# A second one-hot product for the virtual tiles of a graph network, and a shorter gather list

## The chip, the cores and the metric

The kernel runs on one NeuronCore of a Trainium2 chip. The metric is the device time of one execution in microseconds (us). TensorE is called PE here, VectorE DVE, ScalarE ACT, GpSimd POOL and SyncE SP, as in the profile.

## What is computed

Three GraphSAGE layers with maximum aggregation run on 6250 nodes and 200000 edges; the edges are sorted by destination, and low destination numbers have many edges. Cut to what matters:

```
def _sage_conv(x, src, dst, Wl, bl, Wr):
    agg = jax.ops.segment_max(x[src], dst, num_segments=x.shape[0])
    agg = jnp.where(jnp.isfinite(agg), agg, 0.0)
    return agg @ Wl + bl + x @ Wr

h = jnp.maximum(_layernorm(x, axis=-1), 0.0)
h = leaky_relu(_sage_conv(h, ...))   # 128 -> 256
h = leaky_relu(_sage_conv(h, ...))   # 256 -> 256
h = leaky_relu(_sage_conv(h, ...))   # 256 -> 128
return x + h
```

For every node, each layer needs the maximum over the feature rows of its sources.

## The kernel before

**Tiles and pairs.** Nodes are cut into 50 tiles of 127. As sources, two neighbouring tiles make a pair, so there are 25 pairs (`NG`). As destinations, tiles become units of 128 columns in four groups (`GROUPS`, L93): group 0 has 24 narrow units, group 1 has 8 virtual units, group 2 has 19 wide units, group 3 has 4 narrow units. The virtual units stand for the first three tiles, whose nodes have so many edges that each node is cut into rows of up to 64 edges (`CUT`); 8 units hold these rows, and after group 1 the class `Joined` takes the maximum over the rows of one node.

**Two ways to fetch a source row.** The first way is a product: for a pair and a unit, a matrix with a single one per column picks one row of the pair, and PE multiplies the pair's features with it, in two parts (`i`) for exactness. A narrow unit takes one edge per pair in this way: the two tiles of the pair (`s`) are two halves of one sum, and DVE takes one maximum of the result into the accumulator (`maxima`, L929). A wide or virtual unit takes one edge per tile: the two halves are separate results, with a maximum each. ACT builds the one-hot matrices from the index bytes with two instructions each (`one_hot`, L897: Square at L902, Relu at L904), for up to 1024 columns at a time (`HOT`). The second way is a list: the edges left over go to one of four lists (`CAPS`, one per group), sorted so that the deepest rows come first. Each entry is a gather, an indirect DMA that POOL issues for 128 rows (`Listed.gather`, L961, the DMA at L970, followed by a short memset at L974 that paces the queue). DVE takes the maxima of the gathered rows (L985, L990), in blocks of eight gathers in layer 0 and of four in layers 1 and 2.

**Order.** The program is one list of steps written out by hand (`steps`, L1110). For each layer and group the 25 pairs are gone through, and within a pair the chunks of the group: 1024 columns per step in layer 0, where a row is 128 features wide, and 512 columns per step in layers 1 and 2, where it is 256. This gives 75, 25, 75 and 25 steps for the four groups in layer 0, and 150, 50, 125 and 25 in layers 1 and 2. A full step has 8 matmuls of 512 columns (L921). Each step's work goes out in one fixed order on each engine: the products of half 0, then what an agenda has for this step (maxima of gathers, the stages of finished nodes, new gathers), then half 1 and the maximum.

**The agenda.** Everything that is not a product is planned on step numbers. The gathers of lists 0 to 2 are spread evenly from the layer's start to six or eight steps before the end of group 2; in layers 1 and 2 a wide or virtual step counts 1.25 and a narrow one 1.0 (`WIDER`). List 3 goes with group 3. The nodes of a group are finished while the next group runs: for each tile its gathered maximum is fetched (L1014), transposed, merged with the accumulator, and multiplied with the weights (`Node`, L997). For the 24 tiles of group 0 one node begins per step in layer 0, and one per two steps in layers 1 and 2, so they fill the steps of group 1. The eight virtual units and their three tiles follow in the first steps of group 2.

**Building the lists.** The edge rows are read and masked; `flag_rows` (L500) marks which edges the products do not take, `pick_rows` (L531) takes them out eight at a time, `rank_rows` (L549) orders the rows by how many are left, `send_row` scatters them. `expand` (L697) finds, for five pairs at a time, the edge a product takes, and `lookups` (L717) turns that into the index bytes (`idx`). For lists 1 to 3 this is done as chores on the agenda during the first 82 steps of layer 0; those of list 1 lie in the first 40.

If a list or a window should turn out too small for the input, counters (`over`) send the program to a slow general path at its end (L1376).

The stages named in the prediction were found by counting the matmuls of L921 in the order of time: 600, 200, 500 and 100 for the four groups of layer 0, and 1200, 400, 1000 and 200 in layers 1 and 2. They are exact to a few us.

Of the kernel before, what the change touches and what calls it, by code (L numbers as in the profile page):

```python
# [35 lines left out]
I32 = mybir.dt.int32  # L36
# [6 lines left out]
P = 128  # L43
# [6 lines left out]
CUT = 64  # L50
# [10 lines left out]
DEEP = (24, 40, 48, 24)  # L61
# [7 lines left out]
def kernel(ctx: ExitStack, tc: tile.TileContext, x, src, dst,  # L69
# [28 lines left out]
    )  # L98
    PLACE, HEAD = {}, []
# [42 lines left out]
    IW = [(len(units) + sum(w == "w" for w, _ in units)) * P for units in GROUPS]  # L142
# [226 lines left out]
    rows_w = edge.tile([P, NW + NV, 2 * CUT], I16, name="rows_w")  # L369
    pos_i = edge.tile([P, NV], I32, name="pos_i")  # L370
# [90 lines left out]
    def rows_of(us):  # L461
        w, i = us[0]
        assert [u for u in us] == [(w, i + j) for j in range(len(us))]
        return (rows_n if w == "n" else rows_w)[:, i : i + len(us), :]
# [35 lines left out]
    def flag_rows(us, S):  # L500
# [23 lines left out]
        one_less = slice(0, J - 1)  # L524
        nc.vector.tensor_scalar(f[:, :, one_less], b[:, :, one_less], 0.0, float(LEAF), op0=OP.not_equal, op1=OP.mult)
# [191 lines left out]
    def lookups(us, least, s, pool, tags=("v", "v8")):  # L717

        n = len(us)
        wide = us[0][0] == "w"  # L720
        v = pool.tile([P, n, NG], BF16, tag=tags[0], name="v", bufs=1 + (tags[0] == "v"))
        nc.vector.scalar_tensor_tensor(v, least, float(P if wide else 2 * P), least, op0=OP.is_lt, op1=OP.mult)
        if s:
            nc.vector.tensor_scalar(v, v, float(P), None, op0=OP.add)
        v8 = pool.tile([NG, n * P], U8, tag=tags[1], name="v8", bufs=1 + (tags[0] == "v"))
        i = 0
        while i < n:
            k = next(k for k, units in enumerate(GROUPS) if us[i] in units)
            m = 1
            while i + m < n and m < 8 and us[i + m] in GROUPS[k]:  # L730
                m += 1
            p = psum.tile([NG, 8, P], BF16, tag=next(turns), name="lk_p")
            for c in range(m):
                nc.tensor.transpose(p[:, c, :], v[:, i + c, :], ident_b)
            part = v8[:, i * P : (i + m) * P]
            nc.scalar.copy(part.rearrange("g (c k) -> g c k", k=P), p[:, :m, :])
            at = GROUPS[k].index(us[i]) + (len(GROUPS[k]) if s else 0)
            nc.sync.dma_start(idx[k][:, at * P : (at + m) * P], part)
            stored[k] += m * P
            i += m  # L740
# [114 lines left out]
    def chunks(layer, k):  # L855

        n = 8 if widths[layer] == P else 4
        units = GROUPS[k]
        for w in "wn":
            us = [i for i, u in enumerate(units) if u[0] == w]  # L860
            for i0 in range(0, len(us), n):
                part = us[i0 : i0 + n]
                yield (HEAD[k] + part[0]) * P, len(part) * P, part[0], units[part[0]][1] if w == "w" else None
# [23 lines left out]
    def parts_of(k):  # L887

        units = GROUPS[k]
        for w in "wn":  # L890
            us = [i for i, u in enumerate(units) if u[0] == w]
            for i0 in range(0, len(us), HOT // P):
                yield us[i0], len(us[i0 : i0 + HOT // P]) * P, len(units) if w == "w" else 0
# [3 lines left out]
    def one_hot(layer, k, g, c, w, odd, s):  # L897

        t, of = idx_q[layer, k, g]
        at = of + (c + (odd if s else 0)) * P  # L900
# [28 lines left out]
    def maxima(step, s, p, acc):  # L929
        layer, k, g, (_, w, c, odd_u) = step  # L930
# [4 lines left out]
        if g == NG - 1 and (odd_u is None or s == 0):  # L935
# [218 lines left out]
    def late_lookups(us, s):  # L1154
        got = {}
        for g0 in range(0, NG, BATCH):
            def part(g0=g0):
                if g0 == 0:
                    got[0] = made.tile([P, len(us), NG], I16, tag="least", name="least", bufs=2)
                expand(us, CUT if us[0][0] == "w" else CB, g0, s, got[0], S_acc)  # L1160
# [5 lines left out]
    late_lookups(LISTS[1], 1)  # L1166
    n_soon = len(chores)
# [481 lines left out]
```

## Time and profile before

| what | value |
|---|---|
| time, median of 3 runs | 3579.78 us (3576.79 to 3585.17) |
| the profiled execution's own time | 3583.85 us |
| its span, first to last instruction | 3582.1 us |
| mean granted PE clock | 0.86 of full |
| gathers of the lists (L970) | 1815, that is 605 per layer |
| one-hot matrices (L904) | 1200 |
| matmuls with one-hot matrices (L921) | 7000 |
| maxima of products (L938 and L936) | 1350 |
| moved by DMA | 579.84 MB |

Times in the profile are of one execution. A row of a group gives the line of the kernel, the engine, the operation, the tiles written and read, how often it ran, its busy time and the mean of one, and then how long its engine was idle just before such instructions, and what ended that. A row of the stage table gives a stretch of the span from its start, its length, the busy time of each engine with the number of its instructions, the granted PE clock, the share of the DMA engines' time and the rate in GB/s.

### The profile page before, as it was taken

The numbers are of one execution on the slowest core, as the hardware profiler recorded it, in microseconds if no ns is written. First come the engines' busy times: TensorE is split into PE (matmuls) and PEld (weight loads), VectorE is DVE, ScalarE is ACT, GpSimd is POOL, SyncE is SP. The second block draws the span as 40 slices with busy tenths as digits, with TensorE's granted clock in tenths as the row PEclk, the third lists the DMA queues.
The fourth block names the chain that finished last, engine by engine and source line by source line (L and its number), as shares of the span: only waits on it lengthen the run. The fifth ranks groups of instructions, "written<-read, shape, count | busy, mean of one in ns | idle before, by whom it ended". The sixth has DMA issues, their size and how long they took to land.

```text
span 3582.1 us, 37453 instructions
## 1 busy us (share of the span) xinstructions
PE 2378.9 (66%) x8912; PEld 1680.0 (47%) x8912; DVE 2594.4 (72%) x4077; ACT 2460.1 (69%) x3433; POOL 2837.5 (79%) x4030
## 2 busy tenths in 40 slices
PE   1025632557567567888778687769888777677767
PEld 1013421334334335666555455547666555455545
DVE  6557899987556535666667899955666678799964
ACT  5108952769779758998655587757998856477754
POOL 5578894888888873888876788883888888878884
PEclk9986865769767779999889899989999989899989
DMA  9114320338644366555577665578555567565566
GB/s 288 43 20 111 100 76 14 93 98 265 155 129 125 109 188 184 157 171 159 183 227 233 174 186 175 167 212 281 163 162 165 157 212 239 159 168 171 172 188 195
DMA packets 295272, 579.84 MB, mean 162 GB/s; under 512 B 58529, under 2 KB 155669, under 8 KB 294403
## 3 DMA queue, kind: packets, MB, share of 16 engines
q1 hardware_dynamic: 203331, 347.72, 29.7%
q0 software_dynamic: 91648, 229.44, 24.6%
q8 instruction: 75, 1.23, 0.1%
q14 instruction: 154, 1.26, 0.1%
q10 hardware_dynamic: 64, 0.20, 0.0%
HBM read 486.57 MB, written 90.55 MB: 161 GB/s over the span
## 4 chain that ended last, share of the span: by engine, by line
POOL 27%; DVE 22%; PE 14%; issue 14%; ACT 10%; DMA 10%; another core or an unknown queue 1%; SPq 1%; POOLq 0%; DVEq 0%; ACTq 0%
POOL g L970 18%; DVE acc L938 8%; PE pg L921 8%; POOL pace_t L974 7%; ACT sq L902 6%; DMA g<-table,let 5%; ACT hot L904 3%; PE z_p L1043 2%; DVE g L985 2%; DVE g L990 1%; PE z_p L1045 1%; DVE acc L541 1%; DVE acc L539 1%; DMA agg<-best,end_i 1%
## 5 line engine op out<-in xcount | busy, mean ns | idle before, releaser
L921 PE MATMUL pg<-hot,pair_sb 128*128 128x512 f32 x7000 | 2045.9, 440 | 540.3 <-DVE acc L938 243.4
L970 POOL DMA_INDIRECT g<-table,let x1815 | 1830.8, 1009 | 451.0 <-issue 285.2
L921 PEld LDWEIGHTS pg<-hot,pair_sb 128*128 128x128 f32 x7000 | 1397.5, 212 | 1050.5 <-ACT hot L904 293.7
L938 DVE TENSOR_TENSOR acc<-acc,pg 128x1024 f32<-128x1024 f32 (+3 forms) x1314 | 1488.5, 1161 | 309.0 <-PE pg L921 205.9
L904 ACT ACTIVATE hot<-sq 128x1024 fp32r<-128x1024 bf16 (+2 forms) x1200 | 1126.5, 939 | 367.8 <-PE pg L921 298.4
L902 ACT ACTIVATE sq<-idx_sb,near 128x1024 bf16<-128x1024 uint8 (+2 forms) x1200 | 1218.7, 1016 | 15.5 <-POOL pace_t L974 15.5
L974 POOL MEMSET pace_t<- 128x300 bf16 x1815 | 664.0, 366 | 0.9
L985 DVE TENSOR_TENSOR g<-g 128x1024 f32<-128x1024 f32 (+4 forms) x277 | 290.6, 1049 | 209.9 <-DMA g<-table,let 192.8
L1047 ACT COPY s<-z_p 127x256 f32<-127x256 f32 (+1 forms) x150 | 49.9, 333 | 368.4 <-PE z_p L1045 230.6
L990 DVE TENSOR_TENSOR g<-g 128x256 f32<-128x256 f32 (+3 forms) x355 | 175.7, 495 | 83.1 <-DMA g<-table,let 55.9
L1014 POOL DMA_INDIRECT agg<-best,end_i x141 | 140.5, 997 | 95.2 <-PE aT_p L1030 35.5
L959 ACT ACTIVATE let<-ell 128x4 int32<-128x4 int16 (+3 forms) x516 | 92.8, 189 | 86.9 <-DMA ell<-picks 86.9
L1030 PE MATMUL aT_p<-ident,agg 128*128 128x128 f32 x250 | 57.7, 297 | 141.4 <-DMA agg<-best,end_i 112.2
L1043 PE MATMUL z_p<-wr,hT_in 128*128 128x256 f32 (+1 forms) x500 | 148.6, 418 | 4.6 <-DMA hT_in<-across 4.5
L1036 DVE TENSOR_TENSOR mz<-acc,aT_p 128x256 f32<-128x256 f32 (+1 forms) x141 | 52.4, 371 | 131.3 <-PE aT_p L1030 89.3
L1045 PE MATMUL z_p<-wl,mz 128*128 128x256 f32 (+1 forms) x500 | 121.1, 359 | 8.0 <-DVE mz L1036 3.6
L1030 PEld LDWEIGHTS aT_p<-ident,agg 128*128 128x128 f32 x250 | 34.3, 148 | 170.2 <-DMA agg<-best,end_i 114.6
L605 POOL DMA_INDIRECT picks<-picked,to_i x55 | 59.3, 1078 | 64.7 <-DVE rank_h L581 48.1
L1043 PEld LDWEIGHTS z_p<-wr,hT_in 128*128 128x128 f32 x500 | 86.9, 217 | 34.2 <-issue 12.7
L1045 PEld LDWEIGHTS z_p<-wl,mz 128*128 128x128 f32 x500 | 92.3, 210 | 20.9 <-DVE mz L1036 4.4
L830 PE MATMUL hT_p<-ident,h 128*128 128x128 f32 x200 | 44.9, 309 | 82.8 <-DVE mz L1036 44.3
L348 POOL DMA_INDIRECT win_d<-in_dst_dram,win_i x50 | 52.3, 1046 | 44.0 <-ACT junk_w L353 14.7
(259 smaller groups left out, 1133.5 us busy)
## 6 DMA issues: line engine op xcount, KB each, us to landing
pair_sb<-pair SPq DMA_DIRECT2D x200, 512.0 KB
idx_sb<-idx SPq DMA_DIRECT2D x75, 608.0 KB
g<-table,let POOLq DMA_INDIRECT x1815
idx_sb<-idx SPq DMA_DIRECT2D x75, 384.0 KB
pair_sb<-pair SPq DMA_DIRECT2D x100, 256.0 KB
pair<-pr SPq DMA_DIRECT2D x100, 256.0 KB
idx_sb<-idx SPq DMA_DIRECT2D x75, 256.0 KB
best<-g SPq DMA_DIRECT2D x110, 128.0 KB
```

The lines of the kernel that those rows point to most:

```text
L902: nc.scalar.activation(sq[:, :w], t[:, at : at + w], AF.Square, bias=near[:, s : s + 1], scale=1.0)
L904: nc.scalar.activation(hot[:, :w], sq[:, :w], AF.Relu, bias=1.0, scale=-1.0)
L921: nc.tensor.matmul(to, pr[:, s, i, kk * P : (kk + 1) * P], hot[:, o : o + bw], start=((alone or s == 0) and i == 0), stop=((alone or s == ...
L938: nc.vector.tensor_max(to, to, of)
L959: nc.scalar.activation(let[:, :n], ell[self.k][:, q, j : j + n], AF.Identity, scale=1.0)
L970: nc.gpsimd.indirect_dma_start(out=self.tiles[q, b][:, i, :], out_offset=None, in_=tables[self.layer], in_offset=bass.IndirectOffsetOnAxis ...
L974: nc.gpsimd.memset(pace_t, 0.0)
L985: nc.vector.tensor_max(base[:, : i + 1, :], base[:, : i + 1, :], g[:, : i + 1, :])
L990: nc.vector.tensor_max(base[:, :h, :], base[:, :h, :], base[:, w - h : w, :])
L1014: nc.gpsimd.indirect_dma_start(out=self.agg[:, : self.F], out_offset=None, in_=of, in_offset=bass.IndirectOffsetOnAxis(ap=at, axis=0),)
L1043: nc.tensor.matmul(z_p, self.hT[:, i, :], wr[layer][:, i, :], start=False, stop=False)
L1045: nc.tensor.matmul(z_p, self.m[:, i, :], wl[layer][:, i, :], start=False, stop=(i == K - 1))
```

## The change

The eight virtual units get a second kind of product. `flag_rows` looks, among the edges that the first product leaves over, for one per pair; these go to new rows (`rows_x`) and are masked out of the list. New units `("x", v)` are appended to group 1 for the steps and for the index bytes (`PLANES`), while the lists and accumulators stay with `GROUPS`. An x unit is treated as a narrow one: the two halves are one sum, with one maximum, into the accumulator columns of virtual unit v. The list of group 1 has caps of 22, 15, 14, 12, 11, 9, 2 and 1, together 86, in place of 37, 30, 29, 27, 26, 23, 8 and 1, together 181; its depth falls from 40 to 24, so `pick_rows` runs three rounds per unit there and not five. One more set of `expand` and `lookups` is added to the chores, behind those of list 1.

```
-    (37, 30, 29, 27, 26, 23, 8, 1),
+    (22, 15, 14, 12, 11, 9, 2, 1),
...
-DEEP = (24, 40, 48, 24)
+DEEP = (24, 24, 48, 24)
...
+    EXTRA = [("x", v) for v in range(NV)]
+    PLANES = [units + (EXTRA if k == 1 else []) for k, units in enumerate(GROUPS)]
...
-    IW = [(len(units) + sum(w == "w" for w, _ in units)) * P for units in GROUPS]
+    IW = [(len(units) + sum(w == "w" for w, _ in units)) * P for units in PLANES]
...
+        if wide and us[0][1] >= NW:
+            c, seen = S(1, I32, n, J), S(2, I32, n, J)
+            nc.vector.memset(b[:, :, J - 1 :], 0)
+            nc.vector.tensor_copy(c, b)
+            repeated(seen, c, J)
+            nc.vector.tensor_tensor(b, b, c, op=OP.bitwise_xor)
+            x = rows_of([("x", i - NW) for _, i in us])
+            nc.vector.tensor_scalar(f, b, 0.0, float(PAST), op0=OP.is_equal, op1=OP.mult)
+            nc.vector.tensor_tensor(x, f, r[:, :, :J], op=OP.max)
+            nc.vector.tensor_scalar(f, b, 0.0, float(PAST), op0=OP.not_equal, op1=OP.mult)
+            nc.vector.tensor_tensor(r[:, :, :J], f, r[:, :, :J], op=OP.max)
+            b = c
...
     def chunks(layer, k):
...
-        units = GROUPS[k]
-        for w in "wn":
+        units = PLANES[k]
+        for w in "wnx":
...
-                yield (HEAD[k] + part[0]) * P, len(part) * P, part[0], units[part[0]][1] if w == "w" else None
+                yield part[0] - (NV if w == "x" else 0), len(part) * P, part[0], units[part[0]][1] if w == "w" else None
...
     def maxima(step, s, p, acc):
-        layer, k, g, (_, w, c, odd_u) = step
+        layer, k, g, (c, w, _, odd_u) = step
...
-        if g == NG - 1 and (odd_u is None or s == 0):
+        if g == NG - 1 and c == step[3][2] and (odd_u is None or s == 0):
...
     late_lookups(LISTS[1], 1)
+    late_lookups(EXTRA, 0)
     n_soon = len(chores)
```

The remaining edits carry the new units through `lookups`, `parts_of` and `one_hot`, so that the x columns lie behind the 16 of the virtual units in the index bytes. Group 1 then has 50 steps in layer 0 in place of 25, and 100 in place of 50 in layers 1 and 2; per layer 95 gathers go.

More of the change, by code (lines that the diff above doesn't have):

```diff
@@ L369 @@
     rows_w = edge.tile([P, NW + NV, 2 * CUT], I16, name="rows_w")
+    rows_x = edge.tile([P, NV, CUT], I16, name="rows_x")
     pos_i = edge.tile([P, NV], I32, name="pos_i")
@@ L463, in rows_of @@
         assert [u for u in us] == [(w, i + j) for j in range(len(us))]
-        return (rows_n if w == "n" else rows_w)[:, i : i + len(us), :]
+        return {"n": rows_n, "w": rows_w, "x": rows_x}[w][:, i : i + len(us), :]
     def count_of(us):
@@ L727, in lookups @@
         while i < n:
-            k = next(k for k, units in enumerate(GROUPS) if us[i] in units)
+            k = next(k for k, units in enumerate(PLANES) if us[i] in units)
             m = 1
-            while i + m < n and m < 8 and us[i + m] in GROUPS[k]:
+            while i + m < n and m < 8 and us[i + m] in PLANES[k]:
                 m += 1
@@ L736, in lookups @@
             nc.scalar.copy(part.rearrange("g (c k) -> g c k", k=P), p[:, :m, :])
-            at = GROUPS[k].index(us[i]) + (len(GROUPS[k]) if s else 0)
+            at = NV + PLANES[k].index(us[i]) if us[i] in EXTRA else GROUPS[k].index(us[i]) + (len(GROUPS[k]) if s else 0)
             nc.sync.dma_start(idx[k][:, at * P : (at + m) * P], part)
@@ L887, in parts_of @@
     def parts_of(k):
-        units = GROUPS[k]
-        for w in "wn":
+        units = PLANES[k]
+        for w in "wnx":
             us = [i for i, u in enumerate(units) if u[0] == w]
             for i0 in range(0, len(us), HOT // P):
-                yield us[i0], len(us[i0 : i0 + HOT // P]) * P, len(units) if w == "w" else 0
+                yield us[i0], len(us[i0 : i0 + HOT // P]) * P, len(GROUPS[k]) if w == "w" else 0
     hots, live, done_with = {}, [0], [0, 0]
@@ L899, in one_hot @@
         t, of = idx_q[layer, k, g]
-        at = of + (c + (odd if s else 0)) * P
+        at = of + (c + (odd if s else 0) + (NV if PLANES[k][c] in EXTRA else 0)) * P
         sq = work.tile([P, HOT], BF16, tag="sq", name="sq", bufs=2)
@@ L1159, in part @@
                     got[0] = made.tile([P, len(us), NG], I16, tag="least", name="least", bufs=2)
-                expand(us, CUT if us[0][0] == "w" else CB, g0, s, got[0], S_acc)
+                expand(us, CB if us[0][0] == "n" else CUT, g0, s, got[0], S_acc)
             chores.append((.7 * len(us), part))
```

## The prediction

> **What bounds the kernel now.** I read the page first, then the stage table, then the waits and the order of instructions inside stages.
>
> ```profile
> PE 2378.9 (66%) x8912; PEld 1680.0 (47%) x8912; DVE 2594.4 (72%) x4077; ACT 2460.1 (69%) x3433; POOL 2837.5 (79%) x4030
> ...
> POOL 27%; DVE 22%; PE 14%; issue 14%; ACT 10%; DMA 10%; another core or an unknown queue 1%; SPq 1%; POOLq 0%; DVEq 0%; ACTq 0%
> ```
>
> POOL is the busiest engine and has the largest share of the chain that ended last, but four engines lie between 66% and 79%, so the average decides nothing. The stage table does (columns: stretch, length, then PE, PEld, DVE, ACT, POOL busy, clock, DMA share, GB/s). The rows are, in this order, groups 0, 1 and 2 of layer 0, of layer 1 and of layer 2.
>
> ```profile
> 287.00:743.00 456.00, 224.88 (x653) 141.61 (x654) 404.51 (x1023) 323.69 (x373) 362.50 (x531) 0.71 0.27 75
> 743.00:898.00 155.00, 102.36 (x378) 65.97 (x379) 120.22 (x254) 125.53 (x181) 128.44 (x179) 0.83 0.68 201
> 898.00:1236.00 338.00, 206.01 (x570) 132.54 (x569) 192.29 (x251) 280.87 (x402) 297.03 (x435) 0.72 0.45 128
> 1350.00:1728.00 378.00, 311.37 (x1236) 239.83 (x1236) 241.58 (x263) 339.70 (x408) 295.39 (x431) 0.92 0.55 163
> 1728.00:1958.00 230.00, 177.06 (x675) 126.72 (x673) 162.03 (x190) 123.02 (x183) 173.78 (x243) 0.86 0.72 220
> 1958.00:2344.00 386.00, 294.13 (x1102) 202.38 (x1102) 358.40 (x361) 277.47 (x398) 328.86 (x476) 0.93 0.60 178
> 2465.00:2837.00 372.00, 318.90 (x1295) 247.19 (x1294) 242.17 (x258) 336.36 (x407) 288.53 (x422) 0.95 0.56 168
> 2837.00:3034.00 197.00, 142.00 (x644) 103.25 (x643) 160.61 (x193) 114.58 (x150) 172.35 (x236) 0.92 0.69 221
> 3034.00:3429.00 395.00, 297.00 (x1094) 203.62 (x1094) 357.94 (x360) 272.75 (x385) 341.08 (x488) 0.90 0.57 167
> ```
>
> Group 0 of layer 0 is DVE's (405 of 456 us, the chores). Group 0 of layers 1 and 2 has ACT first (340 of 378) with POOL behind it. Group 2 has DVE at 93% and 91% in layers 1 and 2. POOL's true load is higher than its busy time, since every gather has an idle gap of issue before it:
>
> ```profile
> 1647.28 0.95 POOL L970 DMA_INDIRECT g<-table,let  x1 [0.16 <-issue]
> ...
> 1648.76 0.95 POOL L970 DMA_INDIRECT g<-table,let  x1 [0.17 <-issue]
> ```
>
> One gather to the next is 1.48 us. Two stretches of group 0 in layer 1 show what that does: the early part with all engines, then both parts with the one-hots of L904 alone, then the waits from 1540 to 1728.
>
> ```profile
> 1400.00:1500.00 100.00, 89.14 (x357) 68.95 (x356) 69.94 (x67) 98.53 (x113) 87.55 (x130) 0.95 0.55 158
> ```
>
> ```profile
> 1400.00:1500.00 100.00, 48.93 (x47) 0.95 0.55 158
> 1540.00:1720.00 180.00, 78.45 (x74) 0.94 0.54 159
> ```
>
> ```profile
> DVE g L985 <- DMA g<-table,let: 41.8, 16, 5.4
> PE pg L921 <- DVE acc L938: 28.4, 14, 3.6
> ...
> POOL g L970 <- issue: 18.3, 107, 0.9
> ```
>
> Early, ACT is busy 98.5 of 100 us and makes 47 one-hots, 2.13 us each, one per step: that is ACT's own pace. Later a step takes 180/74 = 2.43 us, because POOL is behind its plan: DVE stands in its queue before a gather that has not landed, and PE behind DVE. So POOL costs about 0.3 us a step here, and when it is relieved ACT is next, only 12% below.
>
> **The change: what it takes away.** 95 gathers per layer, 285 x 1.48 = 422 us of POOL. The gathers of lists 0 to 2 fall from 558 to 463 per layer and are spread over more steps. In layers 1 and 2 the weights sum to 359 before (148 + 50 x 1.25 + 119 x 1.25) and 409 after, so a narrow step gets 1.13 gathers in place of 1.55 and a wide one 1.41 in place of 1.94, 27% fewer. In layer 0 it is 514 over 165 steps against 419 over 190 (44 are issued ahead): 2.2 in place of 3.1.
>
> **What it adds.** Per pair, 8 matmuls in layer 0 and 16 in layers 1 and 2, 1000 in all; 2 one-hots per pair and layer, 150 in all; 25 + 50 + 50 = 125 maxima.
>
> ```profile
> L938 DVE TENSOR_TENSOR acc<-acc,pg 128x1024 f32<-128x1024 f32 x1143 | 1362.0, 1216 | 288.9 <-PE pg L921 197.2 <-issue 53.4 <-PE z_p L1045 15.6
> L902 ACT ACTIVATE sq<-idx_sb,near 128x1024 bf16<-128x1024 uint8 x900 | 1021.2, 1135 | 15.5 <-POOL pace_t L974 15.5
> L904 ACT ACTIVATE hot<-sq 128x1024 fp32r<-128x1024 bf16 x900 | 953.2, 1059 | 306.9 <-PE pg L921 252.9 <-issue 27.7 <-ACT sq L902 1.2
> ```
>
> ACT gets 150 x 2.13 = 320 us; DVE 125 x 1.22 = 152 us; PE about 1000 x 0.25 = 250 us (89.14 us for 357 in the busy stretch above). All of it lies in group 1, while POOL's relief is spread over groups 0 to 2. So the sum goes by stage.
>
> *Layer 0, group 0.* DVE is the bound; the new chores come on top of it. In the order of time these rows are the long step of a pass through `repeated`, the maximum of a round of picking, and one part of `expand`, all for the virtual units:
>
> ```profile
> 289.60 3.08 DVE L485 TENSOR_TENSOR acc<-acc 128x496 int32<-128x496 int32 x5
> ...
> 319.85 0.23 DVE L539 MAX8 acc<-acc 128x8 f32<-128x64 f32 x1
> ...
> 361.62 1.85 DVE L703 TENSOR_SCALAR acc<-rows_w 128x512 int16<-128x512 int16 x5
> 363.51 1.71 DVE L709 TENSOR_TENSOR acc<-acc 128x1280 int16<-128x1280 int16 x3
> 365.25 0.49 DVE L710 TENSOR_REDUCE least<-acc 128x40 int16<-128x320 int16 x1
> ```
>
> Five parts cost 20 us. The new pass of `repeated` with its masks is about 8 us, an estimate from the first row (3.1 us for its five long operations, and a dozen of 0.2 to 0.7 us). Two of five rounds go for 8 units, some 16 x 0.5 = 8 us back (a maximum of 0.23 us and a replacement of about the same). Fewer gather maxima give 10 us back. Net **+8 us**; the bounds are -10 (all gather waits of the stage gone too) and +30 (PE and ACT stand behind the extra lookups).
>
> *Layer 0, group 1.* 25 steps become 50, with two one-hots each: 100 x 2.13 = 213 us of ACT, and the stage's other ACT work is 125.5 - 50 x 2.13 = 19 us. ACT so needs 232 us where 155 stood; at 95%, 245: **+90**. POOL (110 gathers and 24 fetches, about 190 us) and DVE stay below that. Bounds +75 and +110.
>
> *Layer 0, group 2.* POOL's 297 us busy and 0.16 us of issue for each gather fill the 338. After, ACT is next with 281 us, 277 with fewer index conversions, POOL needs about 257: 277 at 96% is 288, **-50**. Bounds -65 and -30.
>
> *Layers 1 and 2, group 0.* 150 steps at ACT's 2.13 us are 320, and the slow start of a layer adds 18 to 25: 345 and 338, **-33 and -34**. Bounds -40 and -15 each.
>
> *Layers 1 and 2, group 1.* Here nodes of group 0 run, one per two steps. One such cycle, from one transpose to the next:
>
> ```profile
> 1901.90 0.44 PE L830 MATMUL hT_p<-ident,h 128*128 128x128 f32 x2 [2.19 <-DVE mz L1036]
> ...
> 1912.14 0.44 PE L830 MATMUL hT_p<-ident,h 128*128 128x128 f32 x2 [2.19 <-DVE mz L1036]
> ```
>
> It takes 10.24 us, of which PE waits 2.19 for DVE. The mean over the stage is 230/25 = 9.2 in layer 1 and 197/25 = 7.9 in layer 2. An x cycle has two maxima fewer (2.4 us of DVE), so that wait can go, but PE's own work (177/25 = 7.1 and 142/25 = 5.7 us) stays: I take 7.6 and 6.5. The 24 nodes need 48 of the 100 steps, 12 cycles of each kind: 202 and 173 us. Then 13 pairs of four steps remain with no node to hide. Per pair ACT needs 4 x 2.13 = 8.5 us, DVE six maxima and five gathers' share, 7.3 + 1.6 = 8.9 us (0.32 us a gather, from the rows below); at 93%, 9.5: 124 us. So 326 against 230 and 297 against 197: **+96 and +100**. Bounds +50 (PE's 177 + 50 x 2 at 99%) and +125.
>
> *Layers 1 and 2, group 2.* DVE is at 93% and 91%. Its gather maxima there, L985 and then L990, for layer 1:
>
> ```profile
> 1958.00:2344.00 386.00, 53.98 (x50) 0.93 0.60 178
> 1958.00:2344.00 386.00, 20.13 (x36) 0.93 0.60 178
> ```
>
> 27% of 74 us is 20 us; 338 us remain, and with POOL out of the way DVE runs at 95%: 356 in both layers, **-30 and -39**. Bounds -45 and -12.
>
> The index bytes of group 1 grow by half:
>
> ```profile
> idx_sb<-idx SPq DMA_DIRECT2D x75, 256.0 KB
> ```
>
> 75 x 128 KB = 9.6 MB more, against 30 MB of gathers less (64 KB each in layer 0, 128 KB later); nothing, since the feature pair is loaded once for twice the steps. Setup, group 3 and the ends of layers see no edit: 0, with 10 us either way.
>
> **Sum:** 8 + 90 - 50 = +48; -33 + 96 - 30 = +33; -34 + 100 - 39 = +27. Together **+108 us** on the profiled execution's 3583.85, that is 3692. The median of the runs lies 4 us below it, so **3688 us**.
>
> **Rivals.** *A, faster:* the x work vanishes in the idle time of PE, ACT and DVE, and every stage runs at its busiest engine, as early group 0 of layer 1 does. The needs after the change are, by the working above, 412, 232 and 277 in layer 0; 320, 277 and 338 in layer 1; 320, 242 and 338 in layer 2 (PE in group 1 of layers 1 and 2: 177 and 142 plus 400 matmuls of 0.25): 2756 us where 2907 stand. At 96% that is 2871, or -36: 3544 us. For it: POOL is on the chain most. Against it: today's stages average lower than that wherever nodes run (77% of 230). It needs group 1 of layers 1 and 2 to cost under +60 each. The Trainium skill, "Perfetto Trace Analysis", section "Identifying the Most-Contended Engine", says to take the engine with the highest occupancy for the bottleneck and relieve it first, which here is POOL and speaks for A. Its section "Optimization Strategy" adds that the most contended engine can change from regime to regime; the stage table agrees with that, another engine leading POOL in six of the nine rows.
>
> *B, much slower:* the order within a step, not an engine, holds group 1, so that an x cycle with a node costs as much as a wide one, and groups 0 and 2 give back half, because gathers then wait for ACT, which converts their indices in its queue. 12 x 1.6 + 12 x 1.4 more for the cycles, half of 186 us not regained: +108 + 36 + 93 = +237, 3817 us. For it: the equal 2.19 us gaps. Against: the pace of 2.13 us early in layer 1.
>
> *C, the change doesn't do what it says:* the shorter list does not hold the edges and the general path runs, which would take many times as long. Nothing in the trace bears on it.
>
> **Chances.** The forecast's case 0.67, A 0.16, B 0.16, C 0.01. The range takes in the bounds and most of the way to A and B: 3565 to 3785 us. A measurement of this kernel can tell about 0.2%, 7 us, from no change. Faster, from A and the lowest part of the forecast's bounds, 0.16; the same 0.04; slower 0.80.
>
> **What would show it.** Right: group 1 lasts about 245, 326 and 297 us; early and late group 0 of layers 1 and 2 both run at about 2.13 us a step with ACT near full; POOL's busy time falls to about 2450 us while the span grows; the share of POOL in the chain falls well below 27% and ACT's rises. Wrong: group 1 of layer 1 under 290 us, or group 0 still at 2.4 us a step with 1.13 gathers in each.

## The result, and the profile after

The changed kernel takes 3552.73 us (median of 4 runs, 3548.71 to 3556.08) where the kernel before takes 3579.6 us (4 runs, 3576.79 to 3585.17) on the same chip. The ratio is 0.9923 with a 95% interval of 0.9905 to 0.994: faster by 27 us. The forecast was slower by 108. The two rows of the page that answer to those shown of before:

```profile
PE 2584.7 (73%) x9920; PEld 1804.1 (51%) x9920; DVE 2692.1 (76%) x4152; ACT 2767.4 (78%) x3662; POOL 2439.2 (69%) x3460
...
DVE 23%; issue 22%; ACT 20%; PE 18%; DMA 8%; POOL 7%; SPq 0%; another core or an unknown queue 0%; DVEq 0%; ACTq 0%; POOLq 0%
```

POOL fell from the busiest engine to the fourth, its share of the chain from 27% to 7%. ACT, PE and DVE did more work, 307, 206 and 98 us more, in less time. The stage table of the changed kernel has the same columns as that of before. Here each stage begins where DVE first writes a new accumulator by a copy. The limits used ahead of the result are not exact to a few us: counted in the trace, the matmuls of L921 begin their groups up to 22 us later (group 0 of layer 1 at 1371.5 us, not 1350). The rows are groups 0, 1, 2 and 3 of layer 0, the same of layer 1, and groups 0, 1 and 2 of layer 2.

```profile
279.50:737.90 458.40, 220.07 (x658) 143.22 (x658) 406.93 (x1036) 316.63 (x349) 290.61 (x424) 0.70 0.26 68
737.90:988.00 250.10, 179.30 (x600) 109.82 (x598) 148.67 (x267) 231.50 (x302) 171.21 (x247) 0.86 0.60 162
988.00:1263.90 275.90, 191.79 (x540) 116.48 (x540) 181.53 (x231) 269.13 (x367) 223.16 (x330) 0.80 0.44 129
1263.90:1368.30 104.40, 71.93 (x257) 41.79 (x258) 45.65 (x105) 83.93 (x166) 58.82 (x79) 0.83 0.79 230
1368.30:1697.00 328.70, 300.28 (x1230) 223.40 (x1229) 227.64 (x230) 321.02 (x363) 226.92 (x332) 1.00 0.53 156
1697.00:1992.50 295.50, 267.50 (x1115) 196.58 (x1115) 235.68 (x265) 239.12 (x311) 200.73 (x286) 0.97 0.74 208
1992.50:2360.40 367.90, 289.54 (x1079) 195.62 (x1078) 342.39 (x342) 274.86 (x381) 268.78 (x384) 0.94 0.53 160
2360.40:2466.10 105.70, 95.92 (x445) 71.78 (x443) 62.77 (x98) 75.87 (x151) 58.87 (x77) 1.00 0.97 320
2466.10:2801.40 335.30, 305.59 (x1251) 227.65 (x1250) 228.30 (x231) 323.66 (x367) 226.89 (x332) 0.99 0.52 154
2801.40:3058.40 257.00, 234.95 (x1066) 175.74 (x1066) 229.44 (x264) 222.10 (x263) 201.06 (x286) 0.99 0.71 201
```

The same cuts in the kernel before, group 3 of layer 0 and group 1 of layers 1 and 2:

```profile
1248.10:1375.30 127.20, 76.89 (x258) 45.52 (x257) 45.81 (x105) 78.49 (x156) 79.98 (x109) 0.74 0.66 197
...
1737.30:1973.30 236.00, 181.53 (x699) 130.00 (x698) 167.64 (x198) 126.61 (x192) 176.85 (x250) 0.86 0.75 228
...
2854.00:3050.50 196.50, 142.74 (x654) 103.76 (x654) 162.82 (x199) 108.40 (x144) 171.55 (x236) 0.91 0.71 228
```

Look at group 1 of layer 1. PE does 86 us more work there, and the stage grows by 59.5 us: the old stage had 54 us in which PE was idle, the new one has 28, and the granted clock went from 0.86 to 0.97. By stage, in us, with the forecast's terms beside them:

| stage | before | after | difference | forecast |
|---|---|---|---|---|
| setup | 294.9 | 279.5 | -15.4 | 0 |
| layer 0: groups 0, 1, 2 | 464.2, 147.4, 341.6 | 458.4, 250.1, 275.9 | -5.8, +102.7, -65.7 | +8, +90, -50 |
| layer 0: group 3 and the layer's end | 127.2 | 104.4 | -22.8 | 0 |
| layer 1: groups 0, 1, 2 | 362.0, 236.0, 394.1 | 328.7, 295.5, 367.9 | -33.3, +59.5, -26.2 | -33, +96, -30 |
| layer 1: group 3 | 118.0 | 105.7 | -12.3 | 0 |
| layer 2: groups 0, 1, 2 | 368.6, 196.5, 403.3 | 335.3, 257.0, 367.4 | -33.3, +60.5, -35.9 | -34, +100, -39 |
| layer 2: end | 128.3 | 128.2 | -0.1 | 0 |

The sum is -28 us on the span where +108 was forecast. Of the 136 us between them, 76 lie in group 1 of layers 1 and 2, 35 in group 3, 17 in groups 0 to 2 of layer 0, 15 in the setup, and some 7 the other way in groups 0 and 2 of layers 1 and 2. The setup took from 272.5 to 294.9 us in kernels that share that of before, so its 15 us are not put down to the change. By these cuts the new pass of `repeated`, 8 us of DVE, lies in the setup and not in group 0, and the setup is shorter all the same. The 60.5 us of group 1 in layer 2 are uncertain too: this profile has there 11 us in which PE stood idle although the profile shows nothing that it waited for, two gaps of 3.8 and 3.9 us among them. In a second profile the stage took 254.5 us, and in a kernel on another chip that leaves it alone, without such gaps, 242.9.

### The profile page after: what moved, and what is told of

It is laid out like the page before. It is cut to its first block, busy times and chain, and to the rows that moved or that the text cites. A ratio compares the mean times of both kernels' runs of the same rounds, so it can differ in the third digit from the quotient of the medians.

```text
span 3554.0 us, 39265 instructions
## 1 busy us (share of the span) xinstructions
PE 2584.7 (73%) x9920; PEld 1804.1 (51%) x9920; DVE 2692.1 (76%) x4152; ACT 2767.4 (78%) x3662; POOL 2439.2 (69%) x3460
## 3 DMA queue, kind: packets, MB, share of 16 engines
q8 instruction: 83, 1.36, 0.2%
## 4 chain that ended last, share of the span: by engine, by line
DVE 23%; issue 22%; ACT 20%; PE 18%; DMA 8%; POOL 7%; SPq 0%; another core or an unknown queue 0%; DVEq 0%; ACTq 0%; POOLq 0%
ACT sq L917 15%; DVE acc L953 13%; PE pg L936 12%; POOL g L985 4%; ACT hot L919 3%; DMA g<-table,let 3%; PE z_p L1058 2%; DMA pair_sb<-pair 2%; PE z_p L1060 2%; POOL pace_t L989 2%; DVE g L1000 1%; DVE g L1005 1%; DVE acc L556 1%; DVE acc L554 1%; ACT let L974 1%
## 5 line engine op out<-in xcount | busy, mean ns | idle before, releaser
L936 PE MATMUL pg<-hot,pair_sb 128*128 128x512 f32 (+1 forms) x8000 | 2270.5, 428 | 524.6 <-ACT hot L919 235.8
L985 POOL DMA_INDIRECT g<-table,let x1530 | 1538.4, 1005 | 831.5 <-ACT let L974 381.9
L936 PEld LDWEIGHTS pg<-hot,pair_sb 128*128 128x128 f32 x8000 | 1527.7, 203 | 1139.2 <-ACT hot L919 462.6
L953 DVE TENSOR_TENSOR acc<-acc,pg 128x1024 f32<-128x1024 f32 (+3 forms) x1439 | 1650.3, 1168 | 523.7 <-PE pg L936 405.8
L919 ACT ACTIVATE hot<-sq 128x1024 fp32r<-128x1024 bf16 (+2 forms) x1350 | 1286.1, 953 | 263.6 <-PE pg L936 198.1
L917 ACT ACTIVATE sq<-idx_sb,near 128x1024 bf16<-128x1024 uint8 (+2 forms) x1350 | 1389.5, 1029 | 15.6 <-DMA idx_sb<-idx 15.5
L989 POOL MEMSET pace_t<- 128x300 bf16 x1530 | 559.5, 366 | 1.0
L1000 DVE TENSOR_TENSOR g<-g 128x1024 f32<-128x1024 f32 (+6 forms) x218 | 219.4, 1006 | 3.6 <-DMA g<-table,let 3.5
L1005 DVE TENSOR_TENSOR g<-g 128x512 f32<-128x512 f32 (+3 forms) x351 | 173.0, 493 | 10.2
L1060 PEld LDWEIGHTS z_p<-wl,mz 128*128 128x128 f32 x500 | 90.0, 206 | 22.8 <-issue 8.9
L620 POOL DMA_INDIRECT picks<-picked,to_i x55 | 57.8, 1050 | 34.6 <-DVE rank_f L597 18.7
L724 DVE TENSOR_TENSOR acc<-acc 128x960 int16<-128x960 int16 (+4 forms) x145 | 70.1, 483 | 10.2 <-issue 2.6
```

The lines of the kernel that those rows point to most:

```text
L917: nc.scalar.activation(sq[:, :w], t[:, at : at + w], AF.Square, bias=near[:, s : s + 1], scale=1.0)
L919: nc.scalar.activation(hot[:, :w], sq[:, :w], AF.Relu, bias=1.0, scale=-1.0)
L936: nc.tensor.matmul(to, pr[:, s, i, kk * P : (kk + 1) * P], hot[:, o : o + bw], start=((alone or s == 0) and i == 0), stop=((alone or s == ...
L953: nc.vector.tensor_max(to, to, of)
L985: nc.gpsimd.indirect_dma_start(out=self.tiles[q, b][:, i, :], out_offset=None, in_=tables[self.layer], in_offset=bass.IndirectOffsetOnAxis ...
L989: nc.gpsimd.memset(pace_t, 0.0)
```

## The experiments

The theory after the result: the price of the x work was sized rightly, but the shorter list gives time back in places where the forecast booked nothing, inside group 1 of layers 1 and 2 and in group 3. The rival: the x work costs less than forecast, because it runs in idle time. Both kernels of this question leave the other half of the change out.

**The x products with the old list.** The changed kernel with the list of 181 gathers:

```
-    (22, 15, 14, 12, 11, 9, 2, 1),
+    (37, 30, 29, 27, 26, 23, 8, 1),
-DEEP = (24, 24, 48, 24)
+DEEP = (24, 40, 48, 24)
```

> The x products run, but the list of the virtual units keeps its 181 places and its depth of 40, so all 1815 gathers stay (the places that the x products emptied fetch the floor row). Theory S, the forecast's sum by stage: group 1 costs +90, +96 and +100 us, and the gathers, spread over more steps (1.36 per narrow step in layers 1 and 2 in place of 1.55), give back about 83 us in groups 0 and 2: about 3780 us. Theory G, gaps and backlog: a gather maximum in DVE's queue opens a gap on PE in the node cycles of group 1, and POOL's backlog is paid at the start of group 3; the x steps give POOL time to catch up and DVE slack, so group 1 costs about +103, +65 and +65 us, and groups 0, 2 and 3 give back about 110: about 3700 us.

Measured: 3683.34 us against 3580.94, a ratio to before of 1.03 (1.0267 to 1.0334), slower by 102. That is near the 3700 of theory G, but by two misses: group 1 cost +123, +79 and +89 us, 290 together as in theory S (286) and not 233, and groups 0 and 2 alone gave back 159. The groups 0 of layers 1 and 2 took 329.1 and 334.1 us, as short as with the short list: the added steps alone stretch the plan of the gathers (558 over a weight of 409 is 1.36 for a narrow step, where it was 1.55), and then ACT is the limit. What the shorter list itself gives, from this kernel to the changed one, is -21, -19 and -28 us in the three groups 1, -6, -17 and -17 in the groups 2, and -21 in group 3 of layer 0.

**The short list without the x products.** The kernel before, which gathers only the first 86 entries of the virtual list; the edges in the other 95 are left out of the maximum.

```
+TAKEN = CAPS[:1] + ((22, 15, 14, 12, 11, 9, 2, 1),) + CAPS[2:]
...
-            self.seq = [(q, j) for q, m in enumerate(CAPS[k]) for j in range(m)]
+            self.seq = [(q, j) for q, m in enumerate(TAKEN[k]) for j in range(m)]
...
```

> The kernel before, with only the first 86 of the 181 gathers of the virtual list; no x products, so the edges in the 95 places left out are missing from the maximum. It prices POOL's relief alone. Theory S: groups 0 and 2 give back what the forecast booked less a little, as the density is 1.29 per narrow step: about -165 us, 3415 us, with group 1 and group 3 where they were. Theory G: the same, and on top of it group 3 of layers 0 to 2 starts its nodes 10 to 15 us earlier each, and part of the node cycles of 10.24 us in group 1 fall to 7.5 us: about -220 us, 3360 us. A rival, that ACT holds groups 0 and 2 already: -60 us.

Measured: 3320.41 us, 0.9282 (0.9252 to 0.9312), faster by 260. Group 1 of layer 1 and of layer 2 in this kernel:

```profile
1616.90:1827.30 210.40, 170.05 (x702) 123.77 (x700) 162.65 (x198) 134.01 (x197) 145.22 (x202) 0.94 0.81 247
2647.40:2818.80 171.40, 144.20 (x667) 106.28 (x667) 157.12 (x199) 117.42 (x153) 141.41 (x198) 0.95 0.82 247
```

They have the 50 steps and 24 nodes of the kernel before and last 210.4 and 171.4 us, 26 and 25 less. This splits the result in two (us, spans):

| stages | list relief: this kernel less before | forecast of it | x work: changed kernel less this one | forecast of it |
|---|---|---|---|---|
| groups 0 and 2 | -176 | -186 | -24 | +8 |
| group 1, three layers | -48 | 0 | +271 | +286 |
| group 3 and the end | -28 | 0 | -7 | 0 |
| setup | -18 | 0 | +3 | 0 |
| sum | -270 | -186 | +242 | +294 |

The x work costs 100, 85 and 86 us in group 1: nearly what was forecast, so the rival falls for the most part. Without the setup, whose 18 us are scatter, the relief is -252 where -186 was forecast: 48 us came in group 1 and 28 in group 3 and at the end, where nothing was booked. The two halves do not simply add to those of the kernel above: +102 and -260 make -158, not -27. Stretching the plan and shortening the list relieve the same queue, and each is worth less when the other is done: in groups 0 and 2 the added steps alone gave back 159 us, the short list alone 176, both together 200.

**What the x step waits for.** The changed kernel, in which the x steps take the one-hots of the virtual step, so that ACT makes none for them; the x edges are left out of the maximum.

```
-        hot = hots[layer, k, g, c0, s]
+        mine = PLANES[k][c0] not in EXTRA
+        hot = hots[layer, k, g, c0 if mine else 0, s]
...
```

> The kernel after, but the x steps use the one-hot matrices of the virtual step before them and the second half overwrites the first, so the edges of the x rows are left out; the matmuls and the maxima stay, 300 of ACT's instructions go (about 293 us of its time). If ACT is the bound of group 1 in layer 0, as both theories say, that stage falls from 250 to about 185 us. In layers 1 and 2 theory S has DVE as good as ACT at the bound in the steps without nodes (8.9 against 8.5 us a pair), so 0 to -10 us a layer; about 3475 us in all. Rival: the order of the steps holds group 1 and ACT is only full: less than -25 us, 3530 us.

Measured: 3518.06 us, 0.9828 (0.9794 to 0.9863). Its group 1 of layer 0 and of layer 1:

```profile
742.00:950.70 208.70, 157.08 (x604) 109.31 (x602) 146.95 (x267) 136.99 (x213) 163.49 (x233) 0.88 0.71 190
```

```profile
1665.00:1961.00 296.00, 266.30 (x1113) 195.72 (x1113) 235.58 (x264) 138.90 (x218) 206.79 (x291) 0.97 0.73 209
```

In layer 0 the stage loses 41 us with ACT's 94: ACT was the bound, as forecast. It stops at 208.7 and not at the 185 expected, because POOL is full next: its 163.5 us of work, 21 us of issue gaps and one wait of 18.7 us for DVE make 203. In layer 1 ACT loses 100 us and the stage nothing (296 against 295.5; layer 2 258.1 against 257.0). So ACT doesn't hold it there; PE is the busiest, with 266 of 296 us.

**Why the cycles of group 1 became shorter.** In group 1 of layer 1 of the kernel before, most cycles with a node take either 7.5 or 10.2 us. DVE and PE in a long one:

```profile
1816.10 2.35 DVE L938 TENSOR_TENSOR acc<-acc,pg 128x1024 f32<-128x1024 f32 x2 [1.51 <-PE z_p L1045]
1818.37 1.22 DVE L985 TENSOR_TENSOR g<-g 128x1024 f32<-128x1024 f32 x1
1819.50 0.42 DVE L1054 SCALAR_TENSOR_TENSOR h<-s 127x256 f32<-127x256 f32 x1
1819.84 0.41 DVE L1036 TENSOR_TENSOR mz<-acc,aT_p 128x256 f32<-128x256 f32 x1
```

```profile
1801.33 0.69 PE L830 MATMUL hT_p<-ident,h 128*128 128x128 f32 x2 [3.81 <-DVE mz L1036]
...
1811.63 0.44 PE L830 MATMUL hT_p<-ident,h 128*128 128x128 f32 x2 [1.03 <-DVE mz L1036]
...
1813.14 1.13 PE L1043 MATMUL z_p<-wr,hT_in 128*128 128x256 f32 x4
...
1820.31 0.44 PE L830 MATMUL hT_p<-ident,h 128*128 128x128 f32 x2 [2.17 <-DVE mz L1036]
...
1822.42 2.08 PE L1043 MATMUL z_p<-wr,hT_in 128*128 128x256 f32 x4
```

A gather maximum (L985, 1.22 us) stands in DVE's queue ahead of the node's `h` and `mz`. PE, whose next instruction is the node's transpose, waits 2.17 us for it, in place of 1.03 us where no gather maximum stands there. And then its four matmuls of L1043 take 2.08 us in place of 1.13. The reason for that is in the windows of PE in the same kernel, around this gap and around one 19 us earlier, of 3.81 us (after the busy time: granted clock, DMA share, GB/s):

```profile
1797.00:1801.00 4.00, 0.52 (x3) 0.93 0.66 214
1801.00:1807.00 6.00, 5.67 (x14) 0.50 0.84 249
...
1820.00:1821.00 1.00, 0.69 (x4) 0.98 0.59 216
1821.00:1824.00 3.00, 3.00 (x8) 0.50 0.93 241
```

After the gap the granted clock is half for 3 to 6 us. So 1.22 us of DVE cost a cycle 2.7 us: 1.1 us of waiting, and the rest at half clock. The Trainium skill, "TensorE: Matmul & The Clock Gate", section "HAM oscillation — how this bites in real kernels", has the rule that idle gaps of PE above some 3.4 us bring the half clock. The gap of 3.81 us and the value of 0.50 agree with that; the other gap does not, since 2.17 us were enough here. But not every such gap does it. In this stage all ten gaps of 2.17 to 2.19 us were followed by the half clock; in group 1 of layer 2 of the same kernel eight of ten gaps between 1.9 and 3.0 us were not. Around one of 2.96 us that ended at 2941.76:

```profile
2938.50:2941.50 3.00, 0.30 (x2) 1.00 1.01 349
2942.00:2945.00 3.00, 3.00 (x18) 1.00 0.46 126
```

What decides between them is not shown here. Three experiments test what the gaps and the clock cost. The first takes only the clock out: in the kernel before, eight small matmuls whose result nobody reads fill the gap ahead of each node in group 1 of layer 1.

```
+FILL = 8
...
+        if agenda.get((t, TURN)) and before_ and before_[0][:2] == (1, 1):
+            for i in range(FILL):
+                nc.tensor.matmul(p[:, 0, :], ident_b, mask_v[:, :512], start=True, stop=True)
...
```

> The kernel before, with 8 extra matmuls of 512 bf16 columns (their result is overwritten by the next product) ahead of each node's transposes in group 1 of layer 1, where PE waits for DVE; about 1.8 us of work in each of 24 cycles. Theory G: PE no longer idles for 2.2 to 3.8 us there, the clock stays at 1.0, and the cycles of 10.24 us fall to about 8.7: the stage goes from 236 to about 215 us, although work was added. Theory S knows no such gap: extra work on the engine that is busiest there costs 0 to 43 us: 236 to 280 us.

Measured: 3571.0 us, 0.9969 (0.9955 to 0.9982), a gain of 10 us. Two neighbouring nodes of that stage:

```profile
1831.41 1.90 PE L1350 MATMUL pg<-mask_v,ident_b 128*128 128x512 bf16 x8
1833.74 0.44 PE L831 MATMUL hT_p<-ident,h 128*128 128x128 f32 x2 [0.43 <-issue]
...
1835.25 1.13 PE L1044 MATMUL z_p<-wr,hT_in 128*128 128x256 f32 x4
...
1842.42 0.44 PE L831 MATMUL hT_p<-ident,h 128*128 128x128 f32 x2 [0.44 <-issue]
```

PE has 1.90 us more to do for each node and the long cycles are shorter, 8.68 us here. The stage falls from 236.0 to 221.5 us, its clock rises from 0.86 to 0.95. More work on PE made the stage shorter, so the clock is a cost of its own. The second takes the gather maximum out of the node's way, in the kernel before, for all steps:

```
-        act(MAXIMA, ROWS, REST, LINEAR, MERGE, SOONER, GATHER, FETCH)
+        act(ROWS, REST, LINEAR, MERGE, SOONER, MAXIMA, GATHER, FETCH)
```

> The kernel before, with the maxima of gathers put behind the stages of nodes in each step's order, so that in DVE's queue a node's two short operations no longer stand behind a gather maximum. Theory G: PE's gaps of 2.2 to 3.8 us in the node cycles close, its clock stays up, and cycles of 10.24 us become 7.5 to 8.7: group 1 of layer 1 goes from 236 to about 210 us, that of layer 2 from 197 to about 185; the kernel gains 20 to 40 us, about 3550 us. Rival: the gather maxima have to be made somewhere in the cycle and only move the gap to the products: within 8 us of before.

Measured, on a chip where before takes 3539.91 us: 3501.27 us, 0.9892 (0.9867 to 0.9917). Group 1 of layer 1 lasts 199.4 us in place of 236.0. Group 0 of layer 0 grows by 23 us (487.2), and group 1 of layer 2 does not gain (197.0 against 196.5), where 12 us were expected. The third does the same in layers 1 and 2 alone:

```
+        if t < begins[1]:
+            act(MAXIMA, ROWS, REST, LINEAR, MERGE, SOONER, GATHER, FETCH)
+        else:
+            act(ROWS, REST, LINEAR, MERGE, SOONER, MAXIMA, GATHER, FETCH)
```

> The kernel before, with the gather maxima behind the node stages in each step of layers 1 and 2 only (in layer 0 the same order had cost 23 us in group 0, where the list building stands at that rank). Theory G: group 1 of layer 1 about 200 us, as with the order changed everywhere, the rest as before: about 40 us off, ratio 0.988 to 0.990. If the change then still pays when it is put on top (the next kernel), the closed gaps were not what made it pay; if not, they were.

Measured: 3544.39 us against 3577.03, 0.9906 (0.9891 to 0.9921). DVE in a cycle of its group 1, layer 1:

```profile
1809.59 0.42 DVE L1054 SCALAR_TENSOR_TENSOR h<-s 127x256 f32<-127x256 f32 x1
1809.92 0.41 DVE L1036 TENSOR_TENSOR mz<-acc,aT_p 128x256 f32<-128x256 f32 x1
1810.26 1.22 DVE L985 TENSOR_TENSOR g<-g 128x1024 f32<-128x1024 f32 x1
```

The gather maximum now follows the node's two steps, and the stage lasts 201.3 us with all 181 gathers and no x work. So in layer 1 the position of that one instruction was worth 35 us of 236. In layer 2 it is worth nothing, and yet the short list gave 25 us there. POOL's groups say why; they are those of group 1 in layer 2 of the kernel before (busy time, mean ns, idle time before them and its causes):

```profile
L970 POOL DMA_INDIRECT g<-table,let x106 | 110.0, 1038 | 20.9 <-issue 19.8 <-DVE acc L938 0.6 <-ACT hot L904 0.2
L974 POOL MEMSET pace_t<- 128x300 bf16 x106 | 38.7, 365 | 0.1
L1014 POOL DMA_INDIRECT agg<-best,end_i x24 | 23.1, 964 | 4.0 <-issue 3.6 <-DVE acc L938 0.2 <-DVE g L990 0.2
```

Busy time and issue gaps add up to 196.8 us, the whole stage of 196.5: apart from its issue gaps POOL hardly waits, so it is the bound, and fewer gathers are what helps. (A node of layer 2 also has no transpose L830 that could stand behind `mz`.) In layer 1 of the kernel before it still had 35 us of other waits in its 236:

```profile
L970 POOL DMA_INDIRECT g<-table,let x113 | 112.4, 995 | 55.1 <-ACT let L959 35.1 <-issue 18.3 <-ACT hT L832 1.1
```

The new order took just those away, down to the 201 us at which POOL is full there too. So the short list acts twice in group 1: on POOL, and on DVE's queue ahead of the nodes.

There is a third place, the start of the stage. Two waits of PE in the kernel before, from 1737.3 to 1765 (layer 1) and from 2854 to 2882 (layer 2):

```profile
PE aT_p L1030 <- DMA agg<-best,end_i: 14.0, 1, 14.0
```

```profile
PE aT_p L1030 <- DMA agg<-best,end_i: 14.6, 1, 14.6
```

The fetch for the first node stands in POOL's queue behind gathers that are late: in layer 1 it is issued 16.8 us after the stage begins, with eleven gathers ahead of it, in the changed kernel 1.8 us after. Group 1 falls into three parts, told apart by the first matmul of each node's product (L1041, with the bias): the time until that of the first node, the 23 cycles between the 24 nodes, and the rest (us):

| kernel | layer 1: first node, mean cycle, rest | layer 2: first node, mean cycle, rest |
|---|---|---|
| before | 24.3, 9.20, 0.1 | 24.9, 7.45, 0.3 |
| x products, old list | 15.2, 7.88, 118.4 | 16.2, 6.50, 119.4 |
| short list alone | 10.8, 8.68, 0.1 | 12.6, 6.77, 3.0 |
| changed | 8.2, 7.65, 111.3 | 8.5, 6.09, 108.4 |

The start gives 16 us in each of the two layers, and both halves of the change have a part in it and in the shorter cycles.

**The changed kernel with that order, and without.** Two more kernels on the chip of 3577.03 us: the changed kernel as it is,

> The kernel after, unchanged, as the control of the three others on the same chip: ratio to before 0.9923, and a second profile of its stages. If the 15 us by which the setup was shorter in its first profile belong to the change, the setup is again 15 us shorter than that of the kernels built on before; if it is a matter of the execution, it is not.

and with the order of the last diff.

> The kernel after with the same order in layers 1 and 2. Group 1 has fewer gaps left to close (cycles of 7.5 and 6.4 us, a few of 10.2): group 1 of layer 1 falls by 5 to 12 us, the kernel by 10 to 20 us, ratio about 0.988. So the change is worth 28 us on the old order and about nothing on the new one, if the gaps in the node cycles were a part of its gain; if its gain does not depend on them, this kernel is again 28 us below the last one, ratio 0.981.

Measured: 3554.97 us, 0.9943 (0.9922 to 0.9964), and 3532.96 us, 0.9879 (0.9862 to 0.9896). With the old order the change is worth 22 us on this chip, with the new order 11 (3544.39 to 3532.96), each uncertain by some 8 us. That lies between the two outcomes named: about half of what the change gains, another place in DVE's queue gives as well. The setup of the unchanged copy, 282.0 us, is 10 us shorter than that of the kernel with the new order alone, 291.7; whether the change has a part in that stays open.

**What else holds the changed kernel.** Three kernels on the chip of 3539.91 us, each with one edit in the changed kernel. The changed kernel itself was not run there, and even a stage that an edit leaves alone, as group 1 of layer 2 in the second of them, is shorter there (242.9 us) than on the other chips (257.0 and 254.5). So the times of whole kernels say nothing of the edits, and a stage is compared with the others of the three that leave it alone. First, the gathers. The page of the changed kernel has them wait longest for ACT, which converts their indices:

```profile
L985 POOL DMA_INDIRECT g<-table,let x1530 | 1538.4, 1005 | 831.5 <-ACT let L974 381.9
```

In the experiment POOL converts them itself:

```
-            nc.scalar.activation(let[:, :n], ell[self.k][:, q, j : j + n], AF.Identity, scale=1.0)
+            nc.gpsimd.tensor_copy(let[:, :n], ell[self.k][:, q, j : j + n])
```

> The kernel after, with the conversion of the list entries to 32 bits (444 of ACT's instructions, 81 us of its time in the profile after) moved to POOL, where the gather that uses them is queued. If ACT's own time sets groups 0 and 1 (about 38 conversions of 0.1 us net lie in each group 0 of layers 1 and 2), these fall by 5 to 10 us each and the kernel by 15 to 40 us, to about 3525 us. Rival: POOL's waits for ACT (382 us of idle time in the profile after) are idle time of an engine with slack, and a conversion on POOL takes longer than 0.19 us and delays gathers: 0 to +30 us.

Measured: 3480.53 us, 0.9831 (0.9801 to 0.9861). Group 0 of layers 1 and 2 gains 4 and 6 us, group 1 nothing (291.0 against 290.7, 241.9 against 242.9). So the 381.9 us are, in group 1, idle time of an engine that is no longer the bound. Second, in layer 0 DVE makes the one-hots of the x steps with one comparison, in place of two instructions on ACT:

```
+        if layer == 0 and PLANES[k][c] in EXTRA:
+            nc.vector.tensor_scalar(hot[:, :w], t[:, at : at + w], pos[:, s : s + 1], None, op0=OP.is_equal)
...
```

> The kernel after, with the one-hot matrices of the x units built by one DVE comparison each, in layer 0 only (50 matrices; 100 of ACT's instructions go). The stage was 208.5 us where the x units used other matrices and ACT did nothing for them. If ACT is the bound of group 1 in layer 0, the stage falls from 250 to 210 to 220 us (DVE then has 149 + 50 x 1.1 = 204 us), the kernel to about 3515 us. Rival: DVE's comparison stands in its queue behind maxima that wait for PE, so the matrices come late: stage 235 us or more, the kernel within 15 us of 3553.

Measured: 3466.51 us, 0.9797 (0.9769 to 0.9825). Group 1 of layer 0 falls from 247.7 us (the third of these kernels) to 204.3, and group 2 behind it grows from 276.5 to 296.8. The longest wait of PE in that group 2:

```profile
PE vT_p L1112 <- DMA agg_v<-best,end_i: 28.6, 7, 20.4
```

It is a fetch by POOL, whose gathers are now behind their plan: it issues 92 in group 1, where the changed kernel issues 108, and 176 in place of 160 in group 2. Half the gain is handed to the next stage. Third, in layers 1 and 2 a node begins every fourth step, not every second:

```
-            every = 1 if layer == 0 or k == 2 else 2
+            every = 1 if layer == 0 or k == 2 else 4
```

> The kernel after, with the nodes of group 0 begun every fourth step of group 1 in layers 1 and 2, not every second, so that they fill all 100 steps. Nodes make a pair of steps last 6.4 to 7.6 us, pairs without a node last 4.0. If a node's work on PE and DVE can lie beside ACT's in the steps that ACT or DVE bound, group 1 falls from 296 and 257 to about 275 and 245 us, the kernel to about 3520 us. Rival: a node adds its 2.5 to 3 us to the steps it lies in wherever it lies, because it is a chain through all engines in their queues: the stages stay within 5 us; or PE's clock drops more often: slower.

Measured: 3480.4 us, 0.9827 (0.9798 to 0.9856). Group 1 takes 284.7 and 241.0 us against 290.7 and 242.9: next to nothing, as the rival has it. That nodes crowd the first half of group 1 does not cost much.

**All three together.** The changed kernel with the order in layers 1 and 2, the comparison on DVE in layer 0, and the nodes at every fourth step:

> The kernel after with three edits together: the new order in layers 1 and 2, the one-hot matrices of the x units on DVE in layer 0, and the nodes of group 0 on every fourth step in layers 1 and 2. Each alone touches another stage: group 1 of layer 0 about 205 us (group 2 gives 20 of the 45 us back, POOL being behind there), group 1 of layers 1 and 2 some 10 us shorter each: ratio about 0.975. Rival: the nodes spread out and the new order act on the same gaps, so that only one of them counts: 0.979.

Measured: 3491.35 us, 0.9772 (0.9749 to 0.9794). It is 64 us below the changed kernel on the same chip, and faster than both kernels of the study. Group 1 of layer 0 lasts 202.7 us and group 2 299.4, so the trade seen above remains in it. The ratio lies between 0.975 and 0.979 and decides nothing, but group 1 of layer 1 takes 279.7 us, and 280.0 with the new order alone: there the spread nodes add nothing, as the rival has it.

## Why the prediction was wrong

**The step that failed** is "Layers 1 and 2, group 1". It kept the mean cycle of the stage before, 9.2 and 7.9 us, for the 12 wide cycles, and took 7.6 and 6.5 for those with an x step: 202 and 173 us for the part with nodes, 28 and 24 less than the old stage. That part took 184 and 149 us, 52 and 48 less than the old stage: 16 us of it came at the start, where POOL was no longer late, and 36 and 31 in the cycles. Three transposes of layer 1 in the changed kernel:

```profile
1780.14 0.44 PE L845 MATMUL hT_p<-ident,h 128*128 128x128 f32 x2
...
1787.68 0.44 PE L845 MATMUL hT_p<-ident,h 128*128 128x128 f32 x2 [1.05 <-DVE mz L1051]
...
1794.08 0.44 PE L845 MATMUL hT_p<-ident,h 128*128 128x128 f32 x2
```

An undisturbed wide cycle is 7.5 us, an x cycle 6.4; with the long ones that remain, their means are 8.2 and 7.1, where 9.2 and 7.6 were forecast. The mean of 9.2 was mostly a mixture of 7.5 and 10.2, and the long kind came from the gather maxima, of which the added steps and the shorter list together leave 27% fewer per step. PE's gaps of 1.9 to 4 us in group 1 of layer 1 fell from twelve to four. The prediction used that 27% for group 2 and forgot it for group 1, although it had quoted the waits of 2.19 us for `mz`. The filling and the order experiments show what those waits cost in layer 1; in layer 2 POOL had next to no idle time but its issue gaps. That the two stages had different bounds, the prediction did not see. The same step gave the 52 steps without a node 124 us, DVE's need of 116 at 93%. In layer 1, from just behind the last node:

```profile
1884.90:1992.50 107.60, 99.50 (x405) 72.63 (x405) 102.69 (x95) 106.04 (x118) 82.56 (x121) 1.00 0.74 196
```

From the last node's product on, the rest took 111 and 108 us. In this window DVE needed 103 us and was busy for 95%. ACT, at 99%, did not set it: with ACT freed of the x one-hots (the experiment on what the x step waits for) the rest still took 109 and 108 us. Together group 1 is 30 and 40 us shorter than forecast (295.5 and 257.0 against 326 and 297), and in layer 1 6 us more by the cut, since the old stage was 236, not 230.

**The second failed step** is "Setup, group 3 and the ends of layers see no edit: 0". Code is not all that a stage sees; it also inherits a queue. The waits at the start of group 3 of layer 0, before (1248 to 1285) and after (1264 to 1290):

```profile
PE aT_p L1030 <- DMA agg<-best,end_i: 19.4, 2, 18.8
```

```profile
DVE acc L953 <- PE pg L936: 4.5, 3, 2.3
```

Before, POOL came to the end of group 2 behind its plan, and PE waited 18.8 us for the first fetch. After, no wait there is over 2.5 us, and PE no longer waits for that fetch. In the kernel with the old list and x products the wait is still 17.7 us, with the short list alone 5.4: it takes the short list to shorten it, and the x steps, which give POOL more time, to end it. The stage shows the same: it is 2 us shorter with the x products alone, 12 with the short list alone, 23 with both. In layer 1 group 3 is another 12 us shorter, 13 and 11 in the two kernels with one half of the change.

**What held.** Group 0 of layers 1 and 2 came to -33.3 and -33.3, forecast -33 and -34. ACT is the bound there: 98% and 97% busy, with 65 one-hots in 140 us in the late part of layer 1, 2.15 us a step. In layer 1 the size was in part luck: by the matmuls of L921 the old stage lasted 364 us, not 378, and the slow start was not 25 us but 9 (328.7 less 320). Group 1 of layer 0 came to 250.1, forecast 245, with ACT at 231.5 us, forecast 232. Group 2 of layers 1 and 2 came to -26 and -36, forecast -30 and -39. Group 2 of layer 0 gave 66 where 50 was forecast: ACT needed 269 us, not 277, and was 98% busy, not 96. Group 0 of layer 0 was -6, forecast +8, inside its bounds; the forecast's own terms there, 20 + 8 - 8 - 10, make +10. POOL's busy time (2439 us, forecast 2450) and the shares of the chain moved as said, but the span did not grow. Of the two signs named for "wrong", neither showed clearly: group 1 of layer 1 had to fall under 290 us and lasted 295.5, and 289.4 in the second profile. That limit did not mark the sign: the kernel gained with 295.5.

**The rivals.** A gave 3544 us, needed group 1 of layers 1 and 2 under +60 each, and they were +59.5 and +60.5. Its mechanism, each stage at its busiest engine, holds for group 0 of layers 1 and 2 (98% and 97%); over all of group 1 PE reaches 91%. It was the nearest, and deserved more than 0.16. The rule of the Trainium skill, "Perfetto Trace Analysis", section "Identifying the Most-Contended Engine", which the prediction quotes beside A, to relieve the engine with the highest occupancy, had the right sign: the shorter list alone is worth 260 us. What it can't tell is what the 242 us of the x work take back. B fell: the cycles with an x step are shorter than the wide ones, groups 0 and 2 gave back 200 us and not half of 186, and in the changed kernel gathers that wait for ACT cost group 1 of layers 1 and 2 nothing. C did not occur.

## What to carry to other kernels

A mean over a stage with two kinds of cycle is no price: look for the two kinds, ask what makes the long one, and whether the change removes it. Price relief of a queue in every stage that the queue runs through, and at the start of the stage after it, where its backlog is paid: here that start cost 14 to 19 us three times. Before moving work to another engine, try where the short instruction stands in the in-order queue: here one line of order gave more (33 us) than the change (22 us on the same chip).

## What was not expected of the hardware

Gaps of 2.17 to 2.19 us without matmuls, between stretches of dense ones, were ten times out of ten followed by half the granted clock in one stage, for some 3 us, while gaps of 1.03 to 1.05 us never were; in another stage of the same kernel eight of ten gaps of 1.9 to 3.0 us left the clock at full. Matmuls that nobody reads, 1.90 us of them in each gap, kept it up and were worth 14.5 us in the one stage. The setup took 272 to 295 us on the other chips and 240 to 252 us on the chip where the kernel before takes 3539.91 us, so a difference of 15 us there between single executions says nothing.
